# A decoder layer on one core: the first token group loaded by sequence, six products ahead of it

## The chip, the core and the metric

The kernel runs on one core of a Trainium2 chip. The metric is the device time of one execution in microseconds; times are given as the median of several runs, with the lowest and the highest. The engines are named as in the profile: PE is TensorE's matrix multiply and PEld its weight load, DVE is VectorE, ACT is ScalarE, POOL is GpSimd and SP is SyncE, which issues all the DMA transfers here.

## The reference

One decoder layer over 16 sequences of 256 tokens with 512 features, all in float32. It has three parts, each with a residual and a layer norm behind it. Only the first part touches the change:

```python
xn = x * rsqrt(mean(x * x, axis=-1, keepdims=True) + EPS) * w_norm
proj = einsum('bld,td->blt', xn, W_in)
z  = proj[..., :D_INNER]                    # 1024 columns
xi = proj[..., D_INNER:2 * D_INNER]         # 1024 columns
dt = proj[..., 2 * D_INNER:2 * D_INNER + H] # 16, then B and C, 256 each
xc = conv1d(xi, w_conv)                     # 4 taps along the tokens, causal
xi = silu(xc)
dt = softplus(dt + dt_bias)
# a scan over the tokens with 16 x 16 states, driven by dt, the means of xi, B and C
y  = (scan output spread by W_h2i) * silu(z)
out = einsum('bli,di->bld', y, W_out) + residual
```

The second part is a long convolution gated by a context tensor, the third a linear layer with a choice of two out of eight low-rank updates. They follow after all groups of the first part and are the same in both kernels.

## The kernel before

The first part runs over 8 groups of 512 tokens. A group is two sequences of 256 tokens. Its input arrives in two forms: four tiles `xt` of 128 tokens (256 KB each, for the mean square), and `xnT`, the same values with features on the partitions (four chunks of 128 features, 1,024 KB), which the matrix products read. `rms` takes the sum of squares of the tiles, half of them on ScalarE and half on VectorE in the first group; GpSimd raises it to the power of -1/2; `along_tokens` spreads the result along the tokens by two TensorE products into PSUM; `normed` multiplies `xnT` by it and by the weights `wn`, one chunk after the other, on VectorE.

The products of `proj` use a Strassen-like scheme with seven products instead of eight. The left side is a pair of column blocks of a weight matrix (`w_xi`, `w_z`, `w_bc`; a pair has four loaded blocks A11, A12, A22 and one that becomes S3, 512 KB together, and the sums S1 to S4). The right side are the four quarters of `xnT`: "11" and "12" are the first two chunks for the first and the second sequence, "21" and "22" the last two. T1 to T4 (`XT`) are differences of these quarters, so each needs both sequences. `weight_sums` forms S1 to S4 on GpSimd, `first_token_sum` and `other_token_sums` form T1 to T4. In the first group the four are made by VectorE.

A pair's products accumulate in two PSUM banks `al` and `be`. `first_products` runs A11·"11", S1·T1, S2·T2 and S3·T3; then ScalarE copies the first half of `al` to `u`, and VectorE makes three sums from `u`, `al` and `be` (`first_sums`, lines 394 to 396). `last_products` adds A12·"21" onto the first half of `al`, and S4·"22" and A22·T4 onto `be`; `last_sums` follows (lines 406 to 408). Pairs are called x0 to x3 (`w_xi`), z0 to z3 (`w_z`) and b, c (`w_bc`). The loop at line 692 goes through ten pairs, x0, x1, z0, x2, z1, x3, b, c, z2, z3 in the first group. In iteration i the first products of pair i come first, then the last products of pair i - 1; VectorE then does the first sums of pair i ahead of the last sums of pair i - 1. For an x pair `finish_sums` goes on with `mixed`: four taps of the convolution for each of two blocks, the first tap of the odd block on ScalarE (line 625), everything else on VectorE (lines 627 and 629).

In the first group `decays` (softplus and exponential of dt) is spread over iterations 1 to 4. Its logarithm and the silu behind it each make ScalarE load a table. In iteration 2 these stand between the last sums of x1 and x1's `mixed`.

The order of the instructions on every engine is the order in which the code writes them (a manual schedule). Each engine works through its own list in that order and waits at semaphores. Transfers are issued by SP in the order of the code: four `xt`, `wn`, half of `xnT` by chunks, pair 0 of `w_xi`, the other half, pair 1 of `w_xi`, pair 0 of `w_z`, then the rest. There are eight semaphores for transfers, used in turn, so an issue waits for the transfer eight places before it. Three pairs' banks exist: two in `ps_s`, four in `ps_mm`.

Until the first data are there, `idle` runs products of the identity on TensorE: eight ahead of the first `along_tokens`, four after each of the two.

Of the kernel before, what the change touches and what calls it, by code (L numbers as in the profile page):

```python
# [8 lines left out]
F32 = mybir.dt.float32  # L9
AF = mybir.ActivationFunctionType  # L10
ALU = mybir.AluOpType
# [3 lines left out]
P = 128  # L15
# [10 lines left out]
GT = 512  # L26
# [46 lines left out]
def decoder_kernel(  # L73
# [142 lines left out]
    with ExitStack() as s1:  # L216
# [11 lines left out]

        def load_x(g):
            xs = []  # L230
            for t in range(TT):
# [32 lines left out]

        def weight_sums(eng, w, p):

            ins = eng.tensor_tensor(w[:, p, S1], w[:, p, S3], w[:, p, A22], ALU.add)
            eng.tensor_tensor(w[:, p, S2], w[:, p, S1], w[:, p, A11], ALU.subtract)
            eng.tensor_tensor(w[:, p, S3], w[:, p, A11], w[:, p, S3], ALU.subtract)
            eng.tensor_tensor(w[:, p, S4], w[:, p, A12], w[:, p, S2], ALU.subtract)  # L270
# [12 lines left out]
        for p in range(2, NI // 2):  # L283
# [88 lines left out]

        def begin_products(w, p, third):
# [4 lines left out]
            product(al[:, 0:S], w, p, A11, "11", start=True)  # L378
            return al, be

        def first_products(w, p, third, begun=None, between=None):

            al, be = begun or begin_products(w, p, third)
            product(be[:, 0:S], w, p, S1, "T1", start=True)
            if between is not None:
                between()
            product(al[:, S:], w, p, S2, "T2", stop=True)
            product(be[:, S:], w, p, S3, "T3", stop=True)
            return al, be

        def first_sums(al, be, to):
            u = p2.tile([P, S], F32, tag="u", name="u", bufs=3)
            nc.scalar.copy(u, al[:, 0:S])
            nc.vector.tensor_tensor(u, u, al[:, S:], ALU.add)
            nc.vector.tensor_tensor(to[3], u, be[:, S:], ALU.add)
            nc.vector.tensor_tensor(to[3], to[3], be[:, 0:S], ALU.add)
            return u

        def last_products(al, be, w, p):

            product(al[:, 0:S], w, p, A12, "21", upon=True)
            product(be[:, 0:S], w, p, S4, "22", upon=True)
            product(be[:, S:], w, p, A22, "T4", upon=True)
# [45 lines left out]

        def normed(rt, kcs=range(KD)):  # L450
            for kc in kcs:
                nc.vector.scalar_tensor_tensor(
                    xnT[:, kc, :], xnT[:, kc, :], wn[:, kc : kc + 1], rt, ALU.mult, ALU.mult
                )
# [86 lines left out]
        for w, p in ((w_xi, 0), (w_xi, 1), (w_z, 0), (w_xi, 2)):  # L541
            weight_sums(nc.gpsimd, w, p)
# [51 lines left out]
        for g in range(groups):  # L594
# [24 lines left out]

            def mixed(c):  # L620

                xi = xis[c % 4]
                acc = p2.tile([P, GB, S], F32, tag="acc", name="acc", bufs=6)
                if c % 2:
                    nc.scalar.activation(acc, xi[:, :, 3:], AF.Identity, scale=wc[:, c, 3:4])  # L625
                else:
                    nc.vector.tensor_scalar(acc, xi[:, :, 3:], wc[:, c, 3:4], None, ALU.mult)
                for k in range(2, -1, -1):
                    ins = nc.vector.scalar_tensor_tensor(  # L629
                        acc, xi[:, :, k : k + S], wc[:, c, k : k + 1], acc, ALU.mult, ALU.add  # L630
                    )
                mixes.append(ins)
                accs.append(acc)
                silus.append(acc)
# [35 lines left out]
            before = None  # L670
            begun = []

            def finish_products():
                kind, p, al, be, u, to = before
                last_products(al, be, kinds[kind], p)

            def finish_sums(between=None):
                kind, p, al, be, u, to = before
# [12 lines left out]

            for i, (kind, p) in enumerate(order):
# [5 lines left out]
                if i == 6:  # L698
                    ms = [head_means(0)]
                if g == 0 and i == 0:  # L700
                    al, be = first_products(
                        kinds[kind], p, True, None,
                        lambda: begun.append(begin_products(w_xi, order[1][1], False)),
                    )
                else:
                    al, be = first_products(
                        kinds[kind], p, i % 3 == 0, begun.pop(0) if begun else None
                    )
                if i == 8:
                    ms.append(head_means(1))  # L710
                if i == 9:
# [45 lines left out]
                if i == 8:  # L757
# [8 lines left out]
                before = (kind, p, al, be, u, to)  # L766
                if g:
# [1086 lines left out]
```

## Time and profile before

| | us |
|---|---|
| median of 3 runs (lowest to highest) | 1390.34 (1390.28 to 1390.61) |
| the profiled execution | 1390.65 |
| its span in the profile | 1388.9 |
| PE busy in the span | 1376.9 |
| DVE busy | 1185.3 |
| POOL busy | 621.9 |
| ACT busy | 450.5 |

The profile is one execution, and times in it count from the start of its span. A row of the timeline gives the start, the busy time, the engine, the line of the code, the operation, what it writes and reads with its size, and how many such instructions were merged; in brackets stands how long the engine had been idle before and what ended that. A PE product is recorded as two matmuls for each of its two chunks. A row of SPq is the issue of a transfer, not the transfer.

### The profile page before, as it was taken

To read this page: it belongs to the slowest core of one execution; us is meant where nothing else is said; L and a number is where in the kernel's file an instruction comes from. 1 tells how busy PE (TensorE), PEld (TensorE's weight loads), DVE (VectorE), ACT (ScalarE), POOL (GpSimd) and SP (SyncE) were. 2 spreads that over 40 slices of the span, in tenths; PEclk is the share of its full clock that TensorE was granted. 3 is DMA by queue.
4 is the path that set the end of the run, shared out by engine and by line. 5 is a ranking of instruction groups with operands and counts; after the bars stand their busy time and mean duration, and the time that the engine had idled before them with its cause. 6 is when DMAs were issued, how large, how long until landed. Compare 5 with 4: busy or idle time off the path is not lost.

```text
span 1388.9 us, 19584 instructions
## 1 busy us (share of the span) xinstructions
PE 1376.9 (99%) x6967; PEld 933.7 (67%) x6967; DVE 1185.3 (85%) x2272; ACT 450.5 (32%) x977; POOL 621.9 (45%) x850
## 2 busy tenths in 40 slices
PE   8999999999999999999999999999999999999998
PEld 7888788788887887888887345454454544445454
DVE  6988879879788787787875899999999999999996
ACT  2424324243243242432421223332333333333322
POOL 5451021020100201101003668878888788878885
PEclk9999999999999999999999999999999999999999
DMA  8113212212112121121214654455534554354501
GB/s 309 34 39 91 64 54 37 70 38 58 39 42 62 57 56 52 41 53 40 78 24 72 77 69 63 67 69 69 71 65 63 77 76 65 66 69 61 76 28 38
DMA packets 362386, 89.48 MB, mean 64 GB/s; under 512 B 330032, under 2 KB 334512, under 8 KB 362288
## 3 DMA queue, kind: packets, MB, share of 16 engines
q1 hardware_dynamic: 362288, 88.23, 34.0%
q8 instruction: 55, 0.90, 0.3%
q14 instruction: 43, 0.35, 0.1%
HBM read 70.62 MB, written 17.58 MB: 64 GB/s over the span
## 4 chain that ended last, share of the span: by engine, by line
PE 95%; DVE 2%; POOL 1%; issue 0%; DMA 0%; ACT 0%; SPq 0%; POOLq 0%; DVEq 0%
PE mm L364 21%; PE y L1114 15%; PE s L364 14%; PE y L1129 12%; PE s L832 6%; PE mm L832 6%; PE y L1098 4%; PE be L1376 3%; PE al L1376 3%; PE gl L1321 2%; PE xm L640 1%; PE mm L789 1%; PE s L926 1%; PE mm L926 1%; PE al L1348 1%; PE yps L717 1%
## 5 line engine op out<-in xcount | busy, mean ns | idle before, releaser
L1129 PE MATMUL y<-kv 64*64 64x512 f32 x1536 | 179.6, 598 | 0.0
L1170 DVE TENSOR_TENSOR pr<-y,cT 128x1024 f32<-128x1024 f32 x124 | 146.1, 1219 | 34.2 <-PE y L1129 34.1
L193 DVE TENSOR_TENSOR kv<-tr,cT 128x1024 f32<-128x1024 f32 x128 | 149.9, 1213 | 1.8 <-ACT vT L154 1.8
L629 DVE SCALAR_TENSOR_TENSOR acc<-xi,wc,acc 128x512 f32<-128x512 f32 x192 | 143.2, 759 | 7.4 <-ACT acc L625 1.8
L1180 DVE TENSOR_REDUCE red<-pr 128x128 f32<-128x1024 f32 x126 | 147.2, 1208 | 0.1
L1129 PEld LDWEIGHTS y<-kv 64*64 64x64 f32 x1536 | 52.2, 132 | 118.6 <-issue 97.1
L1114 PE MATMUL y<-kv 128*128 128x512 f32 x272 | 128.0, 594 | 0.6 <-DVE pr L1162 0.4
L68 POOL TENSOR_TENSOR rs_a<-ve_a,nhalf 128x1 f32<-128x1 f32 x31 | 17.0, 548 | 247.2 <-DVE ve_a L66 246.9
L1114 PE MATMUL y<-kv,Td 128*128 128x512 f32 x248 | 116.5, 592 | 0.0
L425 POOL TENSOR_TENSOR rstd<-ms,nhalf 128x4 f32<-128x4 f32 (+1 forms) x9 | 8.6, 956 | 228.3 <-DVE ms L423 228.3
L1103 ACT COPY y<-y 64x512 f32<-64x512 f32 x124 | 69.2, 558 | 66.9 <-PE y L1098 64.9
L364 PE MATMUL mm<-XT,w_z 128*128 128x256 f32 x384 | 90.7, 379 | 0.0
L1114 PEld LDWEIGHTS y<-kv,Td 128*128 128x128 f32 x248 | 47.1, 190 | 59.3 <-issue 59.1
L1084 POOL TENSOR_TENSOR xs<-kv 128x512 f32<-128x512 f32 x63 | 80.1, 1272 | 0.0
L364 PEld LDWEIGHTS mm<-XT,w_z 128*128 128x128 f32 x384 | 73.0, 190 | 9.9
L1114 PEld LDWEIGHTS y<-kv 128*128 128x128 f32 x272 | 51.1, 189 | 42.0 <-ACT y L1103 17.4
L364 PE MATMUL mm<-xnT,w_z 128*128 128x256 f32 x288 | 70.7, 382 | 0.0
L1536 POOL TENSOR_TENSOR ol<-o,red 128x512 f32<-128x512 f32 (+1 forms) x32 | 39.5, 1235 | 62.9 <-DVE red L1180 62.9
L257 POOL TENSOR_TENSOR XT<-xnT 128x512 f32<-128x512 f32 x7 | 9.1, 1299 | 129.0 <-PE mm L832 129.0
L1098 PE MATMUL y<-xs,kv 128*128 128x512 f32 x124 | 64.9, 605 | 0.5 <-issue 0.2
L364 PE MATMUL s<-XT,w_xi 128*128 128x256 f32 x256 | 61.0, 380 | 1.1 <-DVE XT L260 0.5
L364 PEld LDWEIGHTS mm<-xnT,w_z 128*128 128x128 f32 x288 | 54.1, 190 | 10.0 <-issue 3.0
(336 smaller groups left out, 3064.7 us busy)
## 6 DMA issues: line engine op xcount, KB each, us to landing
cT<-in_ctxT SPq DMA_DIRECT2D x32, 384.0 KB
kv<-in_toep SPq DMA_DIRECT2D x32, 384.0 KB
xt<-in_x SPq DMA_DIRECT2D x32, 256.0 KB
spread<-both SPq DMA_DIRECT2D x32, 256.0 KB
first<-xt SPq DMA_DIRECT2D x124, 64.0 KB
vT<-first SPq DMA_DIRECT2D x31, 256.0 KB
out<-res SPq DMA_DIRECT2D x31, 256.0 KB
xnT<-in_xT SPq DMA_DIRECT2D x7, 1024.0 KB
```

The source lines that it names most:

```text
L193: last = nc.vector.tensor_tensor(kv[:, q, k * BQ : (k + NL // 2) * BQ], vT[:, q, blks].rearrange("p k (b i) -> p (k b) i", i=NH).unsqueeze ...
L364: nc.tensor.matmul(ps, w[:, p, a, kc, :], Xs[b][:, kc, :], start=start and kc == 0, stop=stop and kc == 1, skip_group_check=upon,)
L629: ins = nc.vector.scalar_tensor_tensor(acc, xi[:, :, k : k + S], wc[:, c, k : k + 1], acc, ALU.mult, ALU.add)
L832: nc.tensor.matmul(ps, own[a][c][:, n * P : (n + 1) * P], w_o[b][c], start=start and c == 0, stop=stop and c == HC - 1, skip_group_check=upon,
L1084: return nc.gpsimd.tensor_tensor(xs[:, q], moving(kv, q, 0), moving(kv, q, 1), ALU.add)
L1098: nc.tensor.matmul(seed, T[:, SHARED_AT, :], xs[:, q], start=True, stop=True)
L1103: nc.scalar.copy(bank_of(y, 2)[b : b + HP], seed[a : a + HP])
L1114: nc.tensor.matmul(bank_of(y, lb), w, moving(kv, q, mb), start=not late and lb not in begun, stop=False, skip_group_check=True,)
L1129: return nc.tensor.matmul(bank_of(y, lb)[cols], T[rows, DIAGONAL_AT, (b - a) * HP : (b - a + 1) * HP], moving(kv, q, lb)[rows], start=star ...
L1170: nc.vector.tensor_tensor(pr.rearrange("p (k b j) i -> p k b j i", k=2, j=NH), y[i].rearrange("p k (b j i) -> p k b j i", j=NH, i=NH), cT[ ...
L1180: nc.vector.tensor_reduce(red[:, q, 2 * i : 2 * i + 2, :].rearrange("p k t -> p (k t)"), pr, AX.X, ALU.add)
L1376: nc.tensor.matmul(ps, a[:, kc, :], w[:, kc, :], start=(start and kc == 0), stop=(kc == 1), skip_group_check=True,)
```

## The change

The first group's tokens are loaded one sequence after the other: two `xt`, the first sequence's half of `xnT` (all four chunks), then A11 and A12 alone of the pairs x0 and x1, then the other two `xt`, A11 and A12 of z0, the second half of `xnT`, and the remaining blocks of the three pairs. The first sequence is scaled as soon as its own mean squares are there. A11·"11" and A12·"21" of x0, x1 and z0 need nothing else and are run in front; ScalarE copies `u` between the two. The idle products are eight and two.

S1 of x1 is formed by VectorE after T4, and S2, S3, S4 of x1 by VectorE after the first sums of x0; GpSimd leaves these four out. In iteration 1 the last products of x0 stand between S1·T1 and S2·T2 of x1. In iteration 2 the odd block's first tap (`scaled`) stands on ScalarE ahead of the two table loads.

```diff
-        xs_next = load_x(0)
+        halves = [slice(b * S, (b + 1) * S) for b in range(GB)]
+        xs_next = load_x(0, range(TT // GB))
+        nc.sync.dma_start(xnT[:, :, halves[0]], xTg[:, :, halves[0]])
         wn = wp.tile([P, KD], F32, name="wn")
         nc.sync.dma_start(wn, w_norm)
...
-        nc.sync.dma_start(xnT[:, 0:2], xTg[:, 0:2, 0:GT])
-        nc.sync.dma_start(w_xi[:, 0, 0:4], Wxi[:, 0])
-        nc.sync.dma_start(xnT[:, 2:4], xTg[:, 2:4, 0:GT])
-        nc.sync.dma_start(w_xi[:, 1, 0:4], Wxi[:, 1])
-        nc.sync.dma_start(w_z[:, 0, 0:4], Wz[:, 0])
+        for p in range(2):
+            nc.sync.dma_start(w_xi[:, p, 0:2], Wxi[:, p, 0:2])
+        xs_next += load_x(0, range(TT // GB, TT))
+        nc.sync.dma_start(w_z[:, 0, 0:2], Wz[:, 0, 0:2])
+        nc.sync.dma_start(xnT[:, :, halves[1]], xTg[:, :, halves[1]])
+        for w, src, p in ((w_xi, Wxi, 0), (w_xi, Wxi, 1), (w_z, Wz, 0)):
+            nc.sync.dma_start(w[:, p, 2:4], src[:, p, 2:4])
...
-        rt = ps_t.tile([P, GT], F32, tag="tr", name="rt")
+        rts = [ps_t.tile([P, S], F32, tag="tr", name="rt") for _ in range(GB)]
         idle(WARM)
-        for b in range(GB):
-            along_tokens(
-                rt[:, b * S : (b + 1) * S], rms(xs_next[b * TT // GB : (b + 1) * TT // GB], True)
-            )
-            idle(WARM // 2)
-        normed(rt, (0, 1))
+        along_tokens(rts[0], rms(xs_next[: TT // GB], True))
+        idle(2)
+        normed(rts[0], range(KD), halves[0])
+        early = []
+
+        def begin(w, p):
+            al, be = begin_products(w, p, not early, True)
+            early.append((al, be, kept(al)))
+
+        def go_on(w, p, n):
+            product(early[n][0][:, 0:S], w, p, A12, "21", upon=True)
+
+        begin(w_xi, 0)
+        rstd = rms(xs_next[TT // GB :], True)
+        begin(w_xi, 1)
+        go_on(w_xi, 0, 0)
+        begin(w_z, 0)
+        along_tokens(rts[1], rstd)
+        go_on(w_xi, 1, 1)
+        go_on(w_z, 0, 2)
+        normed(rts[1], (0, 1), halves[1])
         first_token_sum(nc.vector)
-        normed(rt, (2, 3))
+        normed(rts[1], (2, 3), halves[1])
         other_token_sums(nc.vector)
-        for w, p in ((w_xi, 0), (w_xi, 1), (w_z, 0), (w_xi, 2)):
+        first_weight_sum(nc.vector, w_xi, 1)
+        for w, p in ((w_xi, 0), (w_z, 0), (w_xi, 2)):
             weight_sums(nc.gpsimd, w, p)
...
             def finish_sums(between=None):
-                kind, p, al, be, u, to = before
+                kind, p, al, be, u, to, _ = before
                 last_sums(al, be, u, to, AF.Silu if kind == "z" else AF.Copy)
+                odd = None
                 if between is not None:
+                    odd = scaled(2 * p + 1)
                     between()
...
                 if kind == "x":
                     mixed(2 * p)
-                    mixed(2 * p + 1)
+                    mixed(2 * p + 1, odd)
...
-                if g == 0 and i == 0:
-                    al, be = first_products(
-                        kinds[kind], p, True, None,
-                        lambda: begun.append(begin_products(w_xi, order[1][1], False)),
-                    )
-                else:
-                    al, be = first_products(
-                        kinds[kind], p, i % 3 == 0, begun.pop(0) if begun else None
-                    )
+                begun = early.pop(0) if early else None
+                soon = g == 0 and i == 1
+                al, be = first_products(
+                    kinds[kind], p, i % 3 == 0, begun and begun[:2],
+                    finish_products if soon else None,
+                )
...
-                if before is not None:
+                if before is not None and not soon:
                     finish_products()
                 to = places(kind, p)
-                u = first_sums(al, be, to)
+                u = first_sums(al, be, to, begun and begun[2])
+                if g == 0 and i == 0:
+                    other_weight_sums(nc.vector, w_xi, 1)
```

`kept` is ScalarE's copy of the first half of `al` to `u`, taken out of `first_sums`; `scaled` is the first tap, taken out of `mixed`; `last_products` leaves A12·"21" out where it has been run in front; `normed` takes a range of tokens.

More of the change, by code (lines that the diff above doesn't have):

```diff
@@ L227, in decoder_kernel, with load_x @@
         groups = NTOK // GT
-        def load_x(g):
+        def load_x(g, ts=range(TT)):
             xs = []
-            for t in range(TT):
+            for t in ts:
                 xt = xp.tile([P, D], F32, tag="xt", name="xt")
@@ L263, in other_token_sums, with first_weight_sum, other_weight_sums @@
             eng.tensor_tensor(Xs["T4"], Xs["21"], Xs["T2"], ALU.subtract)
-        def weight_sums(eng, w, p):
-            ins = eng.tensor_tensor(w[:, p, S1], w[:, p, S3], w[:, p, A22], ALU.add)
+        def first_weight_sum(eng, w, p):
+            return eng.tensor_tensor(w[:, p, S1], w[:, p, S3], w[:, p, A22], ALU.add)
+        def other_weight_sums(eng, w, p):
             eng.tensor_tensor(w[:, p, S2], w[:, p, S1], w[:, p, A11], ALU.subtract)
@@ L270, in weight_sums @@
             eng.tensor_tensor(w[:, p, S4], w[:, p, A12], w[:, p, S2], ALU.subtract)
-            return ins
-        xs_next = load_x(0)
+        def weight_sums(eng, w, p):
+            ins = first_weight_sum(eng, w, p)
+            other_weight_sums(eng, w, p)
+            return ins
+        halves = [slice(b * S, (b + 1) * S) for b in range(GB)]
+        xs_next = load_x(0, range(TT // GB))
+        nc.sync.dma_start(xnT[:, :, halves[0]], xTg[:, :, halves[0]])
         wn = wp.tile([P, KD], F32, name="wn")
@@ L371, in product, with begin_products @@
                 )
-        def begin_products(w, p, third):
+        def begin_products(w, p, third, closed=False):
             al, be = [
@@ L377, in begin_products @@
             ]
-            product(al[:, 0:S], w, p, A11, "11", start=True)
+            product(al[:, 0:S], w, p, A11, "11", start=True, stop=closed)
             return al, be
@@ L386, in first_products, with kept, first_sums @@
                 between()
-            product(al[:, S:], w, p, S2, "T2", stop=True)
+            product(al[:, S:], w, p, S2, "T2", stop=True, upon=begun is not None)
             product(be[:, S:], w, p, S3, "T3", stop=True)
             return al, be
-        def first_sums(al, be, to):
+        def kept(al):
             u = p2.tile([P, S], F32, tag="u", name="u", bufs=3)
             nc.scalar.copy(u, al[:, 0:S])
+            return u
+        def first_sums(al, be, to, u=None):
+            u = u or kept(al)
             nc.vector.tensor_tensor(u, u, al[:, S:], ALU.add)
@@ L397, in first_sums, with last_products @@
             return u
-        def last_products(al, be, w, p):
-            product(al[:, 0:S], w, p, A12, "21", upon=True)
+        def last_products(al, be, w, p, whole=True):
+            if whole:
+                product(al[:, 0:S], w, p, A12, "21", upon=True)
             product(be[:, 0:S], w, p, S4, "22", upon=True)
@@ L448, in load_along_tokens, with normed @@
             )
-        def normed(rt, kcs=range(KD)):
+        def normed(rt, kcs=range(KD), tokens=slice(0, GT)):
             for kc in kcs:
+                part = xnT[:, kc, tokens]
                 nc.vector.scalar_tensor_tensor(
-                    xnT[:, kc, :], xnT[:, kc, :], wn[:, kc : kc + 1], rt, ALU.mult, ALU.mult
+                    part, part, wn[:, kc : kc + 1], rt, ALU.mult, ALU.mult
                 )
@@ L618, in decoder_kernel, with scaled @@
             Bs, Cs = [], []
-            def mixed(c):
+            def scaled(c):
                 xi = xis[c % 4]
@@ L627, in mixed @@
                     nc.vector.tensor_scalar(acc, xi[:, :, 3:], wc[:, c, 3:4], None, ALU.mult)
+                return acc
+            def mixed(c, acc=None):
+                xi = xis[c % 4]
+                acc = acc or scaled(c)
                 for k in range(2, -1, -1):
@@ L670, in decoder_kernel @@
             before = None
-            begun = []
             def finish_products():
-                kind, p, al, be, u, to = before
-                last_products(al, be, kinds[kind], p)
+                kind, p, al, be, u, to, whole = before
+                last_products(al, be, kinds[kind], p, whole)
             def finish_sums(between=None):
-                kind, p, al, be, u, to = before
+                kind, p, al, be, u, to, _ = before
                 last_sums(al, be, u, to, AF.Silu if kind == "z" else AF.Copy)
+                odd = None
                 if between is not None:
+                    odd = scaled(2 * p + 1)
                     between()
@@ L765, in decoder_kernel @@
                         next(w_sums)
-                before = (kind, p, al, be, u, to)
+                before = (kind, p, al, be, u, to, not begun)
                 if g:
```

## The prediction

> **What bounds the kernel now.** I read the page's first part, then the chain that ended last.
>
> ```profile
> PE 1376.9 (99%) x6967; PEld 933.7 (67%) x6967; DVE 1185.3 (85%) x2272; ACT 450.5 (32%) x977; POOL 621.9 (45%) x850
> ...
> PE 95%; DVE 2%; POOL 1%; issue 0%; DMA 0%; ACT 0%; SPq 0%; POOLq 0%; DVEq 0%
> ```
>
> TensorE is busy for 99% of the span and carries 95% of the chain. A change therefore pays only by what it takes from TensorE's few gaps, and costs whatever gap it opens. The waits of TensorE alone say where the gaps are; columns are total us, times, longest.
>
> ```profile
> PE rt L431 <- POOL rstd L425: 1.2, 2, 0.7
> PE s L364 <- DVE XT L260: 0.5, 1, 0.5
> PE s L364 <- DVE XT L257: 0.5, 1, 0.5
> ```
>
> With the first wait for the identity (1.8 us) this is nearly all of it, and these rows lie in the first 16 us. So the only thing to win is the start, a few us of 1389. The timeline of the first 20 us shows what sets it:
>
> ```profile
> 6.57 0.69 DVE L417 SCALAR_TENSOR_TENSOR sq<-xt 128x512 f32<-128x512 f32 x1 [1.11 <-DMA xt<-in_x]
> ...
> 8.23 0.33 SPq L288 DMA_DIRECT2D w_dt<-in_WdtT  x1
> ...
> 9.14 1.41 DVE L452 SCALAR_TENSOR_TENSOR xnT<-xnT,wn,rt 128x512 f32<-128x512 f32 x2 [1.59 <-PE rt L431]
> 9.51 0.78 SPq L291 DMA_DIRECT2D dtb<-in_dt_bias  x1
> 9.56 0.73 POOL L267 TENSOR_TENSOR w_xi<-w_xi 128x256 f32<-128x256 f32 x1 [1.22 <-DMA w_xi<-in_Wxi]
> 10.90 0.63 SPq L293 DMA_DIRECT2D A<-in_A_log  x1
> ...
> 12.18 2.89 SPq L295 DMA_DIRECT2D w_z<-in_Wz  x3
> ...
> 15.21 1.21 DVE L263 TENSOR_TENSOR XT<-xnT,XT 128x512 f32<-128x512 f32 x1
> ...
> 15.83 1.17 POOL L270 TENSOR_TENSOR w_xi<-w_xi 128x256 f32<-128x256 f32 x1
> ...
> 16.34 0.41 DVE L394 TENSOR_TENSOR u<-u,s 128x256 f32<-128x256 f32 x1
> ...
> 17.30 0.42 DVE L396 TENSOR_TENSOR xi<-xi,s 128x256 f32<-128x256 f32 x1
> ...
> 18.95 1.24 PE L364 MATMUL s<-xnT,w_xi 128*128 128x256 f32 x5
> ```
>
> Three readings. First, transfers land in queue order: from the ninth on, each issue on SP waits until the transfer eight places before it has landed. So the issues at 8.23, 9.51, 10.90 and 12.18 tell when 1,538, 2,050, 2,562 and 3,074 KB had arrived (first half of xnT, w_xi pair 0, second half of xnT, w_xi pair 1); GpSimd's first weight sum, at 9.56, agrees. Second, from the square of the last x tile (6.57) to the scaling of xnT (9.14) takes 2.57 us. Third, TensorE runs without a gap from 16.36 on; until then it waits for the DVE sums T1 to T4.
>
> The next stretch shows how little room DVE has once TensorE is running:
>
> ```profile
> 21.75 0.42 DVE L407 TENSOR_TENSOR xi<-u,s 128x256 f32<-128x256 f32 x1 [1.64 <-PE s L364]
> ...
> 34.62 0.71 ACT L625 ACTIVATE acc<-xi,wc 128x512 f32<-128x512 f32 x1
> ...
> 35.36 2.33 DVE L629 SCALAR_TENSOR_TENSOR acc<-xi,wc,acc 128x512 f32<-128x512 f32 x3 [1.75 <-ACT acc L625]
> ...
> 37.60 0.41 DVE L394 TENSOR_TENSOR u<-u,s 128x256 f32<-128x256 f32 x1
> ...
> 38.29 1.89 PE L364 MATMUL s<-xnT,w_xi 128*128 128x256 f32 x8
> ...
> 38.58 0.42 DVE L396 TENSOR_TENSOR xi<-xi,s 128x256 f32<-128x256 f32 x1
> ```
>
> At 38.29 TensorE takes up the last three products of pair x2, which write into the banks that DVE has just read: A12·"21" waits for DVE's first sum (37.60 to 38.01), S4·"22" (39.15, one product later) for the third, which ends at 39.00. The slack is 0.15 to 0.28 us. DVE itself had lost 1.75 us before that (35.36), waiting for ScalarE's tap (34.62), which stood behind two table loads.
>
> **The change, step by step.** One product is 0.86 us (three in 16.36 to 18.95).
>
> *Loads.* Eight transfers of xnT and weights replace five, of the same bytes; half of xnT and two 256-KB blocks of w_xi now stand ahead of xt 2 and 3. The last xt therefore has 2,050 KB up to and with it, which arrived at 9.48 before: 3 us later than now. The first half of xnT and wn have about the 1,026 KB that let the square of the last xt run at 6.57. w_xi's two blocks come at some 7.5 and 8.2, w_z's at 10.2, xnT's second half (2,818 KB) at 11.5. SP's three extra issues (0.45 us each) are hidden by data still queued; if the queue ran dry, they would cost 1.4.
>
> *First half of the tokens.* Squares of xt 0 and 1 and the first rt are as now, so the four scalings of the half start at 7.05 (now 8.39 + 0.71 is the second rt; the first ends at 7.03). A half-size scaling is 0.28 shorter (0.70 at 512 columns; 0.42 for a DVE sum of 256). TensorE then runs six products in front: A11 of x0, x1, z0 and A12 of the same, from 7.6 to about 13.8, with the second rt between them. ScalarE's copy of x0 now stands ahead of its square of xt 2, done by 9.7, so it is not late. The six products fill time that was idle; two idle matmuls stay of eight, and no gap of TensorE below is over 1.2 us.
>
> *Second half.* The square of xt 3 at 9.55 and 2.57 us give the scaling at 12.12 (9.14 before). Two scalings (1.44 now, 0.88 halved): T1 at 13.0. T1 0.98, two scalings 0.87, T2 1.08, T3 1.14 apart as before: T2 14.85, T3 15.93, T4 17.07, and the next DVE work 18.20 (16.34 before, +1.86).
>
> *Weight sums of x1 on DVE.* The first stands between T4 and x0's sums. No row shows one on DVE. The nearest is T4 (15.21): 1.21 us for 512 columns, with GpSimd's sum at 15.83 stretched from 0.73 to 1.17. Scaled by size this is 0.6. The Trainium skill, "SBUF — State Buffer", section "SBUF: two separate sides", says that a DVE instruction with two SBUF inputs and a GpSimd instruction reading SBUF exclude each other for the whole instruction. Then only DVE's own part shrinks: 1.21 - 0.28 = 0.93. GpSimd is busy with twelve sums from 12 to 24 us here, so I take 0.93; by the scaled row the end would be 0.33 earlier. Bounds: 0.35 and 1.15. x0's sums then start at 19.05 and end at 20.43 (17.72 before: +2.7). The three other sums (2.8 us) fit into the wait for x1's products, until 23.2; without that cover they would cost all of it. GpSimd loses four sums, which nobody waited for; it starts when w_xi 0's second block lands (3,074 KB, 12.2), and S2 is there by 14.5, needed at 16. Its later sums (w_z 1, w_xi 3) start behind the taps, up to 3.3 us later: w_z 1's first at 31, TensorE needs it after 35.
>
> *TensorE.* T3 of x0 at 17.25; T1 of x1 waits for the weight sum, 19.24; x0's S4·"22", moved up between x1's products, waits for x0's third sum: 20.54 (19.81 before). From there to x2's A12·"21" it took 18.48 us with 20 products; now 19 lie there, so 17.62: it is reached at 38.16. All six early products have bought 0.13 us.
>
> *DVE behind it.* x0's last products go ahead of x1's T2 and T3, but on DVE x1's first sums stay ahead of x0's last sums. They wait for T3 of x1 (20.54 + 4 products = 23.99), so x0's last sums begin at 25.05 (21.75 before: +3.3). What follows up to x2's first sum took 15.85 us, 1.75 of it the wait for the tap. The tap now stands ahead of both loads and that wait goes: 14.10, so 39.15 instead of 37.60. ScalarE's copy that this sum needs is late next: 35.23 + 3.3, done at 38.9, 0.25 ahead.
>
> *The new stall.* TensorE stands ready at 38.16; A12·"21" can start at 39.15 + 0.41 + 0.11 = 39.67, and S4·"22" after the third sum (39.15 + 0.98 + 0.42 + 0.11 = 40.66). It was 39.15. So TensorE is **1.5 us later** from here. DVE is late by as much, so the next slots (banks of z0 at 40.9, first sums of z1 at 43.5) keep their room, and with TensorE full to the end nothing gives the time back.
>
> Sum: span 1388.9 + 1.5 = 1390.4. The profiled execution took 1390.65, 1.75 around its span and 0.31 over the median 1390.34. So 1392.15 on its own scale, **1391.8** against the median: 0.1% slower, which is within 0.2% (2.8 us), about what a measurement of this kernel can tell from no change.
>
> **The rivals.**
> *Slower by over 0.2%: the transfers in 1-KB pieces.* Both halves of xnT are now read in runs of 1 KB instead of 2. Every us by which the last xt lands after 9.5 moves the second rt, T1 to T4, x0's sums and the stall one for one. For: no large transfer of the first 10 us has pieces so small. Against: w_o is read in 1-KB runs, and the windows show 258 to 348 GB/s from 22 to 28 us, when it was under way, against 293 to 386 from 2 to 10 us. If the 512 KB took twice their 1.4 us, the end is 1391.8 + 1.4 = 1393.2. It decides from 1.3 us of delay, x2's first sum after 40.4.
> *The gain stands.* If the weight sum costs its bound of 0.35 and DVE makes up the rest in the taps, so that x2's first sum is in time, TensorE keeps 0.13 + 0.58 = 0.7: 1389.6. Against: it would need DVE 1.5 us earlier on work whose durations the trace shows.
> *The tap brings nothing.* ScalarE's order is changed as said, but if its copy of x2 came 0.5 us later than reckoned, it would replace the tap as the wait: 1392.1; with the whole 1.75 lost, 1393.6.
>
> **How the numbers follow.** Forecast, 1391.0 to 1392.6 with the weight sum between its bounds and 0.4 for landings: 0.72. Gain stands, or half of it: 0.12, nearly all within 0.2%. Late transfers: 0.10; tap lost: 0.06, of both about three quarters over 1393.1. Range 1389.7 to 1393.4. Faster by over 0.2% would need 2.8 us, more than the start still holds without its loads: 0.02. Slower: 0.12. Same: 0.86.
>
> **What would show it.** Second scaling of xnT near 12.1; six products before 14; DVE's first weight sum near 0.9; x0's S4·"22" waiting for DVE near 20.5; no DVE wait for the tap of x1; in TensorE's waits a new row on a DVE sum of x2, 1.5 to 2.5 us. I am wrong if TensorE has no gap after 21 us, or if the last xt lands away from 9.5.

## The result, and the profile after

The changed kernel took 1392.42 us in the median of 21 runs (1391.58 to 1394.20), the kernel before 1390.61 us in 21 runs on the same chip (1390.17 to 1391.76). The ratio is 1.0015 with a 95% interval of 1.0009 to 1.0021: slower by 1.8 us, within 0.2%. In the experiments below one run of e9 (1598.07 us, granted clock 0.85) and one of the kernel before (1444.40 us) had a lower granted clock and are left out of the ratios and of e9's median. The profiled execution took 1391.98 us with a span of 1390.0, 1.1 us more than the span before.

The page's rows on busy time and on the chain that ended last:

```profile
PE 1376.8 (99%) x6955; PEld 932.9 (67%) x6955; DVE 1186.7 (85%) x2280; ACT 450.1 (32%) x977; POOL 618.4 (44%) x846
...
PE 94%; DVE 3%; issue 0%; POOL 0%; ACT 0%; POOLq 0%; DVEq 0%
```

TensorE's work is the same (1376.8 us busy against 1376.9), so the loss is in its gaps: PE's share of the chain has gone from 95% to 94%, DVE's from 2% to 3%. TensorE's waits in the changed kernel (total us, times, longest):

```profile
PE s L374 <- DVE u L408: 1.1, 1, 1.1
PE mm L374 <- DVE w_xi L266: 0.9, 1, 0.9
PE s L374 <- DVE XT L260: 0.7, 1, 0.7
...
PE rt L446 <- POOL rstd L440: 0.4, 1, 0.4
```

Before, the rows after the first identity were two waits for GpSimd's rstd (1.2) and two for T1 and T2 (0.5 each), all in the first 16 us. Now the first row is a wait of 1.15 us at 39 us, for VectorE's first sum of x2 (L408, `u`). The forecast for that row was 1.5 to 2.5 us. The second is for S1 of x1, which VectorE now makes (L266). The timeline of the start:

```profile
6.02 1.22 PE L446 MATMUL rt<-ident,rstd 128*128 128x128 f32 x4 [0.43 <-POOL rstd L440]
...
7.88 1.15 PE L374 MATMUL s<-xnT,w_xi 128*128 128x256 f32 x4
...
9.50 0.69 DVE L432 SCALAR_TENSOR_TENSOR sq<-xt 128x512 f32<-128x512 f32 x1 [0.57 <-DMA xt<-in_x]
...
11.46 0.61 PE L446 MATMUL rt<-ident,rstd 128*128 128x128 f32 x4
...
12.11 0.87 DVE L468 SCALAR_TENSOR_TENSOR xnT<-xnT,wn,rt 128x256 f32<-128x256 f32 x2 [1.63 <-PE rt L446]
12.77 1.03 PE L374 MATMUL mm<-xnT,w_z 128*128 128x256 f32 x4
13.01 0.69 DVE L257 TENSOR_TENSOR XT<-xnT 128x512 f32<-128x512 f32 x1
...
16.58 1.21 DVE L263 TENSOR_TENSOR XT<-xnT,XT 128x512 f32<-128x512 f32 x1
17.71 0.94 DVE L266 TENSOR_TENSOR w_xi<-w_xi 128x256 f32<-128x256 f32 x1
18.57 0.41 DVE L408 TENSOR_TENSOR u<-u,s 128x256 f32<-128x256 f32 x1
```

The six early products run from 7.88 to 13.80, in time that was idle. But the second scaling starts at 12.11 (9.14 before), T4 at 16.58 (15.21) and x0's first sums at 18.57 (16.34). The first row is read again further down: four small matmuls that took 0.71 us before took 1.22 here. The stretch in which the loss is fixed:

```profile
24.59 0.41 DVE L422 TENSOR_TENSOR xi<-u,s 128x256 f32<-128x256 f32 x1
...
25.25 0.48 DVE L659 TENSOR_SCALAR acc<-xi,wc 128x512 f32<-128x512 f32 x1
25.76 4.56 DVE L667 SCALAR_TENSOR_TENSOR acc<-xi,wc,acc 128x512 f32<-128x512 f32 x6
...
33.52 0.72 ACT L657 ACTIVATE acc<-xi,wc 128x512 f32<-128x512 f32 x1
34.27 1.28 ACT L498 ACT_TABLE_LOAD   x1
...
34.00 4.56 DVE L667 SCALAR_TENSOR_TENSOR acc<-xi,wc,acc 128x512 f32<-128x512 f32 x6
38.58 0.42 DVE L408 TENSOR_TENSOR u<-u,s 128x256 f32<-128x256 f32 x1
39.06 2.11 PE L374 MATMUL s<-xnT,w_xi 128*128 128x256 f32 x8 [1.15 <-DVE u L408]
...
40.04 0.73 PEld L374 LDWEIGHTS s<-xnT,w_xi 128*128 128x128 f32 x4 [0.25 <-DVE xi L410]
...
49.01 1.13 PE L374 MATMUL s<-xnT,w_bc 128*128 128x256 f32 x4
```

ScalarE's tap now stands ahead of the table load (33.52, 34.27), and VectorE's six taps run without the 1.75 us hole they had. Even so x2's first sum comes at 38.58 (37.60 before), and TensorE, ready at 39.06 - 1.15 = 37.91, waits for it, and for the third sum once more (0.25). The first product of pair b (the last row) follows at 49.01. The kernel before had it at 48.02:

```profile
48.02 1.13 PE L364 MATMUL s<-xnT,w_bc 128*128 128x256 f32 x4
```

So 0.99 of the 1.1 us have been lost by there, and nothing gives them back.

### The profile page after: what moved, and what is told of

Same layout as the page of the kernel before. It is cut to its first block, busy times and chain, and to the rows that moved or that the text cites. A ratio compares the mean times of both kernels' runs of the same rounds, so it can differ in the third digit from the quotient of the medians.

```text
span 1390.0 us, 19573 instructions
## 1 busy us (share of the span) xinstructions
PE 1376.8 (99%) x6955; PEld 932.9 (67%) x6955; DVE 1186.7 (85%) x2280; ACT 450.1 (32%) x977; POOL 618.4 (44%) x846
## 4 chain that ended last, share of the span: by engine, by line
PE 94%; DVE 3%; issue 0%; POOL 0%; ACT 0%; POOLq 0%; DVEq 0%
PE mm L374 20%; PE y L1152 15%; PE s L374 13%; PE y L1167 12%; PE s L870 6%; PE mm L870 6%; PE y L1136 4%; PE be L1414 3%; PE al L1414 3%; PE gl L1359 2%; PE xm L678 1%; PE mm L827 1%; PE s L964 1%; PE mm L964 1%; PE al L1386 1%; DVE acc L667 1%
## 5 line engine op out<-in xcount | busy, mean ns | idle before, releaser
L68 POOL TENSOR_TENSOR rs_a<-ve_a,nhalf 128x1 f32<-128x1 f32 x31 | 16.9, 546 | 248.0 <-DVE ve_a L66 247.6
L374 PE MATMUL mm<-XT,w_xi 128*128 128x256 f32 x256 | 60.7, 379 | 0.9 <-DVE w_xi L266 0.9
```

What stands on the lines that cost most here:

```text
L374: nc.tensor.matmul(ps, w[:, p, a, kc, :], Xs[b][:, kc, :], start=start and kc == 0, stop=stop and kc == 1, skip_group_check=upon,)
```

## The experiments

Each kernel is the changed kernel with the edit shown, except where it says "before". The kernel before had medians of 1390.79, 1390.72 and 1390.64 us in the three sets of runs (e1 to e4, e5 to e8, e9 to e12). The three sets ran on three different chips, each beside the kernel before; the changed kernel was not run again with them. "x0's first sums", "x0's last sums" and "x2's first sum" are the starts on VectorE in the profiled execution.

Two things limit what can be read. The intervals of nearly all ratios below overlap that of the changed kernel (1.0009 to 1.0021); only e3's lies above it and e5's below. The readings therefore rest on single profiled executions, and in these the loads land at different times though their order is the same: the square of the last `xt` started at 9.50 in the changed kernel, and at 9.01 (e3), 9.79 (e2), 9.82 (e1), 9.93 (e4) and 10.04 (e7) in others. In e7, which only adds two idle products at the start, the second scaling came 0.50 later than in the changed kernel, x2's first sum 0.53 later and the span is 0.5 longer. So the landing of the last `xt` is passed on to the end, and where a few tenths matter the distance from the second scaling (12.11 in the changed kernel) is given too.

**e1: the sums of x1 on GpSimd again.**

```diff
-        first_weight_sum(nc.vector, w_xi, 1)
-        for w, p in ((w_xi, 0), (w_z, 0), (w_xi, 2)):
+        for w, p in ((w_xi, 0), (w_xi, 1), (w_z, 0), (w_xi, 2)):
...
-                if g == 0 and i == 0:
-                    other_weight_sums(nc.vector, w_xi, 1)
```

> The changed kernel with all four weight sums of x1 back on GpSimd, between those of x0 and z0; all else as changed. Theory (VectorE's chain sets TensorE's place): the first weight sum (0.94 us in the profile) no longer stands between T4 and x0's sums, so x0's first sum starts near 17.7 instead of 18.57, x2's first sum near 37.7 instead of 38.58, and TensorE's wait there (1.15 us) moves forward with it: the span is 0.8 to 0.9 us shorter than the changed kernel's 1390.0. Rival (the later landing of the last xt alone sets the delay, VectorE's sums are hidden): no change within 0.2 us.

Measured: 1392.17 us (13 runs, 1391.41 to 1393.62), ratio to before 1.0011 (1.0003 to 1.0019), span 1389.7. x0's last sums came at 23.99, 0.60 earlier than in the changed kernel; x2's first sum at 38.56, 0.02 earlier. Counted from the second scaling (12.38 here) these are 0.87 and 0.29. Either way 0.58 was given back in between. GpSimd, which has four sums more, is now still at work on w_xi 2 when VectorE does the taps of x0. The timeline of e4 (below) shows this at its clearest; in e1 the taps took 0.69 and 4.91 us where the changed kernel has 0.48 and 4.56. So the delay of x0's sums by the first weight sum is real and of the size expected, but taking it away alone is worth 0.3 us of span, not 0.8: GpSimd's four sums were not free where they were.

**e2: last products of x0 behind all of x1's first products, as before.**

```diff
-                soon = g == 0 and i == 1
+                soon = False
```

> The changed kernel with x0's last products put back behind all first products of x1. Theory: TensorE no longer waits for x0's third sum at 20.0, T2 and T3 of x1 come 1.7 us earlier, VectorE does x1's first sums in that time and waits only for T4 of x0; x0's last sums start 0.4 to 0.8 us earlier than 24.59, and x2's first sum with them. Span 0.4 to 0.8 shorter than 1390.0. Rival (moving x0's last products forward is what lets the taps of x0 start, so undoing it delays them): x0's last sums later than 24.59, span 0.5 or more longer.

Measured: 1392.05 us (21 runs, 1391.56 to 1394.36), ratio 1.0012 (1.0005 to 1.0018), span 1389.8. x2's first sum came at 38.39, 0.19 earlier, and the span was shorter by as much: half of the smallest gain expected. Part of this is the load: counted from the second scaling (12.36 here), x0's last sums came 0.47 earlier and x2's first sum 0.44, at the low end of the 0.4 to 0.8 expected. From its timeline:

```profile
24.37 0.42 DVE L422 TENSOR_TENSOR xi<-u,s 128x256 f32<-128x256 f32 x1 [0.77 <-PE s L374]
```

VectorE was done with x1's first sums at 23.60 (24.67 in the changed kernel), but x0's last products now stand behind x1's on TensorE, and VectorE waits 0.77 us for them. That wait takes back most of what the order gives.

**e4: both together.**

> Both of the first two edits in one: x1's weight sums on GpSimd, and x0's last products behind x1's first. Theory: the two shares add up, 1.3 to 2.3 us less than the changed kernel's span, so 1387.7 to 1388.7, at or under the kernel before (1388.9). Rival (the loads set the delay): the same as the changed kernel.

Measured: 1391.29 us (13 runs, 1390.61 to 1392.12), ratio 1.0004 (0.9996 to 1.0012), span 1389.1. From its timeline, to be held against the two tap rows at 25.25 and 25.76 shown above:

```profile
22.62 0.42 DVE L422 TENSOR_TENSOR xi<-u,s 128x256 f32<-128x256 f32 x1 [0.85 <-PE s L374]
...
23.29 0.71 DVE L658 TENSOR_SCALAR acc<-xi,wc 128x512 f32<-128x512 f32 x1
...
24.04 5.61 DVE L666 SCALAR_TENSOR_TENSOR acc<-xi,wc,acc 128x512 f32<-128x512 f32 x6
24.55 1.17 POOL L270 TENSOR_TENSOR w_xi<-w_xi 128x256 f32<-128x256 f32 x1
25.69 1.17 POOL L271 TENSOR_TENSOR w_xi<-w_xi 128x256 f32<-128x256 f32 x1
...
29.56 0.41 DVE L408 TENSOR_TENSOR u<-u,mm 128x256 f32<-128x256 f32 x1
```

x0's last sums are 1.97 us earlier than in the changed kernel (22.62 against 24.59), and 2.36 counted from the second scaling (12.50 here). From the first tap to z0's first sum VectorE then took 29.56 - 23.29 = 6.27 us, against 30.24 - 25.25 = 4.99 there: 1.28 is given back, 0.69 remains, and x2's first sum is at 37.90. The GpSimd rows beside the taps show why: 1.17 us each instead of the 0.73 of one left alone, and six taps 5.61 instead of 4.56. The two engines hold each other up there. The span is 0.9 us shorter than the changed kernel's, where 1.3 to 2.3 were expected.

**e3: the tap behind the table loads, as before.**

```diff
-                    odd = scaled(2 * p + 1)
```

> The changed kernel with ScalarE's tap of x1 put back behind the two table loads. Theory: VectorE waits for the tap again, about 1.8 us, x2's first sum comes near 40.4 instead of 38.58, and TensorE's wait for it grows from 1.15 to about 3 us: span 1.7 to 1.9 longer, 1391.8. Rival (VectorE has room here, the tap is hidden): the wait shows on VectorE, the span stays within 0.3.

Measured: 1395.95 us (5 runs, 1395.48 to 1397.58), ratio 1.004 (1.0027 to 1.0052), span 1393.0, which is 3.0 more than the changed kernel. From its timeline, and below it a row of its windows (stretch and length, then busy time and instructions of PE, PEld, DVE, ACT and POOL, then the granted clock of TensorE, DMA share and GB/s):

```profile
37.91 2.33 DVE L667 SCALAR_TENSOR_TENSOR acc<-xi,wc,acc 128x512 f32<-128x512 f32 x3 [1.99 <-ACT acc L657]
...
40.62 1.65 PE L374 MATMUL s<-xnT,w_xi 128*128 128x256 f32 x3 [3.12 <-DVE u L408]
```

```profile
40.00:46.00 6.00, 5.38 (x18) 4.50 (x19) 5.69 (x14) 3.35 (x6) 5.53 (x8) 0.72 0.00 0
```

The wait for the tap is back with 1.99 us, and TensorE's wait grows by the same, 1.15 to 3.12. That is about the 1.8 that was expected. The rest is the clock: the granted clock is 0.72 over these 6 us, which is half speed for 3.4 of them (0.28 of 6, doubled). The two products at 40.62 took 3.41 us from start to start, against 1.95 in the changed kernel, so the clock cost 1.46. With the 1.97 of waiting that is 3.4; the loads of this execution came 0.4 earlier, which leaves the 3.0 of its span. The medians of the spans, 1393.7 and 1390.4, differ by 3.3. The tap's place is thus worth 3.0 to 3.4 us in the changed kernel, where the next experiment finds nothing for it in the kernel before.

**e5: before, with the tap ahead of the loads and nothing else.**

```diff
                 if between is not None:
+                    odd = scaled(2 * p + 1)
                     between()
```

> The kernel before, with only ScalarE's tap of x1 moved ahead of the two table loads. Theory (TensorE bounds, and VectorE was just in time in the kernel before): VectorE's wait of 1.75 us goes, x2's first sum comes near 35.9 instead of 37.60, but TensorE takes up x2's last products at 38.3 as before: the time stays within 0.3 us of before. Rival (the tap is a gain of its own): 1 us or more less than before.

Measured: 1390.88 us (13 runs, 1390.21 to 1391.49), ratio 0.9999 (0.9991 to 1.0007), span 1388.6. From its timeline:

```profile
35.60 0.42 DVE L394 TENSOR_TENSOR u<-u,s 128x256 f32<-128x256 f32 x1
...
38.02 1.24 PE L364 MATMUL s<-xnT,w_xi 128*128 128x256 f32 x5
```

x2's first sum comes 2.0 us earlier than before (37.60), and TensorE gets to its products at 38.02 as it would have anyway: it is 0.27 earlier, as was all of this run from x0's first sums on (16.07 against 16.34). The sum is done at 36.02, so VectorE has 1.9 us to spare here. The changed kernel spends that room, and more, on the later start of its chain.

**e6 and e7: the idle products.** e6 has none ahead of the first products; e7 has ten instead of eight ahead of the first `along_tokens`.

```diff
-        idle(WARM)
+        idle(WARM + 2)     # e7; e6 has neither idle(WARM) nor idle(2)
```

> The changed kernel without the ten idle products. Theory on the changed kernel's scatter (7 of 21 runs lie 1.9 us above the rest): TensorE's clock is at half speed until it has been busy for a while; with no idle products the six products in front run at half speed (1.7 us each instead of 0.86), the second rt, which stands behind four of them, comes 1 to 3 us later than 11.46, and the end moves by as much: 1393 to 1395 us in most runs. Rival (the clock has nothing to do with the scatter): the second rt at 11.5, 1392.4 as the changed kernel.

> The changed kernel with ten instead of eight idle products ahead of the first rt, so that TensorE is busy without a gap from 1.8 to the first rt. Theory on the scatter (late clock at the start): the runs at 1393.8 and more go, all lie between 1391.5 and 1393. Rival (the scatter comes from the clock falling after the wait at x2's last products, or from elsewhere): a fifth to a third of the runs still lie 1.9 us above the others.

Measured for e6: 1393.84 us (9 runs, 1393.63 to 1395.28), ratio 1.0024 (1.0014 to 1.0033), span 1393.0. From its timeline:

```profile
7.93 2.05 PE L374 MATMUL s<-xnT,w_xi 128*128 128x256 f32 x4 [0.75 <-DMA w_xi<-in_Wxi]
9.77 1.91 PE L374 MATMUL mm<-xnT,w_xi 128*128 128x256 f32 x4
11.47 1.92 PE L374 MATMUL s<-xnT,w_xi 128*128 128x256 f32 x4
13.18 1.24 PE L374 MATMUL mm<-xnT,w_z 128*128 128x256 f32 x4
14.26 0.61 PE L446 MATMUL rt<-ident,rstd 128*128 128x128 f32 x4
```

Three products and a part of the fourth ran at half speed, and the second `along_tokens` (L446), which stands behind four of them in TensorE's order, starts at 14.26 instead of 11.46. From there every step of the chain is later by about 3 us, to the end of this execution; the median of the nine spans, 1391.9, is 1.5 above that of the changed kernel.

Measured for e7: 1392.42 us (21 runs, 1391.95 to 1393.29), ratio 1.0012 (1.0006 to 1.0019), span 1390.5. The median is that of the changed kernel, but the spread is not. The 21 spans of the changed kernel fall in two groups, 14 from 1389.5 to 1390.5 and 7 from 1391.7 to 1392.1. Two more idle products leave only the first kind (all 21 from 1390.0 to 1391.3), and no idle products only the second or worse (all nine from 1391.7 up). That points to runs in which the clock became full late: the change cut the idle products from 16 to 10, and the kernel before, with 16, has no such group in the three sets (134 spans, all from 1388.2 to 1389.8). But the changed kernel was not run beside e7, and the count is not all of it: of the other kernels with ten idle products e9 has 4 of 12 spans above a gap of 0.8 us and e2 has 3 of 21 above a gap of 1.0, but e1 and e4 have none in 13 each. No run of the upper group was profiled; that its products were slow is inferred from e6 and e7.

The profiles do show that the clock comes up at different times. Before, the first `along_tokens` was this row:

```profile
6.32 0.71 PE L431 MATMUL rt<-ident,rstd 128*128 128x128 f32 x4 [0.75 <-POOL rstd L425]
```

In the changed kernel it took 1.22 us (the first row of the timeline of the start), so it ran cold, at half speed, and so did the two idle products behind it (0.61 us in e7):

```profile
7.03 1.06 PE L543 MATMUL mm<-ident 128*128 128x128 f32 x4
```

In e1, e2 and e4, which have the same products up to there, it took 0.71. The first product, at 7.88, took 1.15 us in the changed kernel and 1.13 in e7, so there the clock was full just in time. (The clock column of the windows shows 1.00 in all of this stretch, also where products ran at half speed, so it is the durations that are read.)

**e8: the last `xt` ahead of the weight blocks.**

```diff
+        xs_next += load_x(0, range(TT // GB, TT))
...
         for p in range(2):
             nc.sync.dma_start(w_xi[:, p, 0:2], Wxi[:, p, 0:2])
-        xs_next += load_x(0, range(TT // GB, TT))
-        nc.sync.dma_start(w_z[:, 0, 0:2], Wz[:, 0, 0:2])
         nc.sync.dma_start(xnT[:, :, halves[1]], xTg[:, :, halves[1]])
+        nc.sync.dma_start(w_z[:, 0, 0:2], Wz[:, 0, 0:2])
...
+        rstd = rms(xs_next[TT // GB :])
         begin(w_xi, 0)
-        rstd = rms(xs_next[TT // GB :], True)
         begin(w_xi, 1)
+        along_tokens(rts[1], rstd)
         go_on(w_xi, 0, 0)
-        begin(w_z, 0)
-        along_tokens(rts[1], rstd)
         go_on(w_xi, 1, 1)
+        begin(w_z, 0)
         go_on(w_z, 0, 2)
```

> The changed kernel with the last two xt loaded ahead of the weight blocks (and the second half of xnT ahead of z0's block), both squares on ScalarE, and the second rt ahead of the A12 products. Theory (the landing of the last xt sets T1 to T4, x0's sums and the stall at x2): the second scaling starts near 11.0 instead of 12.11, x2's first sum near 37.6 instead of 38.58, span 0.6 to 1.0 shorter than 1390.0. Rival (x0's and x1's products on TensorE set x0's last sums): the scaling comes earlier, x2's first sum and the span stay within 0.3.

Measured: 1392.78 us (21 runs, 1390.89 to 1395.80), ratio 1.0014 (1.0008 to 1.0021), span 1392.2. From its timeline:

```profile
9.41 2.04 PE L374 MATMUL s<-xnT,w_xi 128*128 128x256 f32 x4 [2.36 <-DMA w_xi<-in_Wxi]
11.24 1.91 PE L374 MATMUL mm<-xnT,w_xi 128*128 128x256 f32 x4
12.95 1.06 PE L446 MATMUL rt<-ident,rstd 128*128 128x128 f32 x4
```

and from its windows:

```profile
7.05:8.40 1.35, 0.00 (x0) 0.00 (x0) 1.15 (x3) 0.54 (x1) 0.00 (x0) 1.00 1.01 319
8.40:8.60 0.20, 0.00 (x0) 0.00 (x0) 0.20 (x2) 0.20 (x3) 0.00 (x0) 0.77 1.04 394
8.60:15.20 6.60, 5.79 (x16) 4.84 (x17) 1.59 (x5) 1.37 (x4) 2.98 (x5) 0.50 1.04 391
```

Moving `xt` up moved `w_xi` back: the first product waits until 9.41, 2.36 us after the last idle product, and now runs at half speed, although the clock had been full before the wait (the last four idle products, at 6.44, took 0.61 us; cold, four took 1.06 in the changed kernel). The windows give the moment: the granted clock fell at 8.5, after 1.5 us of waiting, and was half for 6.8 us, until 15.3. The second `along_tokens` at 12.95 is later than in the changed kernel, not earlier. The fastest runs (1390.89, span 1389.0) may show what the order gives without the clock; none of them was profiled. So the experiment missed its question, and e10 to e12 put it again with enough idle products to bridge that wait.

**e9: VectorE takes x0's last sums and the taps of its even block ahead of x1's first sums.**

```diff
+            def half_sums():
+                kind, p, al, be, u, to, _ = before
+                last_sums(al, be, u, to, AF.Copy)
+                odd = scaled(2 * p + 1)
+                mixed(2 * p)
+                return lambda: mixed(2 * p + 1, odd)
...
+                if soon:
+                    rest = half_sums()
                 u = first_sums(al, be, to, begun and begun[2])
...
-                if before is not None:
+                if soon:
+                    rest()
+                elif before is not None:
```

> The changed kernel with VectorE's order changed alone: in iteration 1 the last sums of x0 and the taps of its even block stand ahead of the first sums of x1, the taps of its odd block behind them. Theory (x0's last sums were late only because x1's first sums, which wait for T3 of x1, stood ahead of them): x0's last sums start near 22.2 instead of 24.59, x0's taps end 1.2 us earlier, x2's first sum near 37.4 instead of 38.58, span 0.9 to 1.2 shorter than 1390.0. Rival (the order on VectorE is neutral, what counts is its sum of work): x2's first sum within 0.3 of 38.58.

Measured: 1391.85 us in the median of 12 runs (1391.35 to 1393.30), ratio 1.0011 (1.0003 to 1.002). In the profile TensorE's products took 1.18 us instead of 1.03, so only VectorE's stretch is read from it: from x0's first sums (19.05) to x2's first sum (38.32), without an idle row, it took 19.27 us, against 20.01 in the changed kernel. The order is worth 0.7 us on VectorE (0.9 to 1.2 expected); the time is 0.6 lower, which the intervals cannot tell from no change.

**e10 to e12: the parts together.** All three have the loads and order of e8 and twenty idle products (`idle(WARM + 2)`, `idle(10)`). e10 adds the edits of e1 and e2, e11 that of e9, e12 those of e9 and e1.

> The loads and TensorE order of e8 with the edits of e4, and ten idle products before and ten behind the first rt, so that TensorE has no gap until its first product. Theory: the clock stays up, the second scaling starts near 11.0, x2's first sum 1.3 us earlier than in e4 (37.90), near 36.7, span 1387.6 to 1388.4, which is 0.5 to 1.2 under the kernel before (1388.9), and the runs keep within 1 us. Rival (TensorE's own products from 9 us on set x0's last sums): 1388.5 to 1389.

> The loads and TensorE order of e8 with the idle products of e10 and VectorE's order of e9; the weight sums of x1 stay on VectorE. Theory: fewer collisions with GpSimd than in e10, x0's last sums near 21: x2's first sum near 36.6, span 1387.8 to 1388.6. Rival: the first weight sum (0.94) in the way gives it all back, 1389.

> As e11, with the weight sums of x1 on GpSimd. Theory: 0.9 us off VectorE and TensorE ahead of x0's sums, 0.5 of it given back by taps that collide with GpSimd (as e1 showed): span 1387.5 to 1388.3, the shortest of all. Rival: GpSimd's sums are late for x1's products, 1388.5 or more.

Measured: 1390.90 (1390.46 to 1391.33), 1390.91 (1390.45 to 1391.46) and 1390.82 us (1390.43 to 1391.52), 13 runs each; ratios to before 1.0002 (0.9994 to 1.001), 1.0002 (0.9994 to 1.0011) and 1.0001 (0.9993 to 1.001). The loss of the change is gone and its two groups of runs too, but none is faster than the kernel before: the spans were 1388.9, 1389.1 and 1389.1 in the profiles, where 1387.5 to 1388.6 were expected. What the six early products can do is seen in e10, from its timeline:

```profile
9.11 1.03 PE L374 MATMUL s<-xnT,w_xi 128*128 128x256 f32 x4
...
10.84 0.61 PE L446 MATMUL rt<-ident,rstd 128*128 128x128 f32 x4
...
22.57 0.42 DVE L422 TENSOR_TENSOR xi<-u,s 128x256 f32<-128x256 f32 x1 [0.85 <-PE s L374]
...
38.30 2.11 PE L374 MATMUL s<-xnT,w_xi 128*128 128x256 f32 x8 [1.60 <-DVE u L408]
```

TensorE stood ready for x2's last products at 38.30 - 1.60 = 36.70, 1.6 us ahead of the kernel before. It starts them when that did (38.29), because VectorE's sum was not there. And e10's second `along_tokens` is still at 10.84 (8.39 before): it waits behind two products whose weights come at 9.1, because the loads ahead of them hold `xt` now. The rival named for e10 came true as well: its second scaling is 1.02 us earlier than in e4 (11.48 against 12.50), but x0's last sums start at 22.57 (22.62 in e4), since VectorE waits there for TensorE. TensorE's six early products start later with their weights, and x1's products start at 18.06 (18.11 in e4). Loading `xt` earlier thus only changes which engine is late. The kernels side by side:

| | x0's first sums | x2's first sum | between | VectorE's waits in it | TensorE ready |
|---|---|---|---|---|---|
| before | 16.34 | 37.60 | 21.26 | 4.36 (1.75 of it for the tap) | 38.29 |
| e5 | 16.07 | 35.60 | 19.53 | 2.62 | 38.02 |
| changed | 18.57 | 38.58 | 20.01 | 1.34 | 37.91 |
| e1 | 18.00 | 38.56 | 20.56 | 3.39 | 37.32 |
| e4 | 18.12 | 37.90 | 19.78 | 1.81 | 36.74 |
| e10 | 17.60 | 37.82 | 20.22 | 2.39 | 36.70 |
| e11 | 18.68 | 37.96 | 19.28 | 0 | 38.15 |
| e12 | 17.70 | 37.95 | 20.25 | 2.46 | 38.12 |

"Between" starts with x0's first sums, which need T1 to T4 and so both sequences. It is 19.3 to 20.6 us in all kernels that load by sequence, but not for one reason. Where VectorE makes the sums of x1 (changed, e11) it has 18.7 and 19.3 us of work and waits little; where GpSimd makes them it has 17.2 to 18.0 us of work and waits 1.8 to 3.4 us for TensorE's products. To use e10's 1.6 us, x2's first sum would have to start at 36.2, and x0's first sums 19.3 to 20.2 us ahead of that, at 16.0 to 16.9; they came at 17.60. In e11 and e12 TensorE is held up instead: in e11, as in the changed kernel, it waits for the first weight sum on VectorE and for x0's third sum (0.26 and 0.17 us); in e12 it waits for x0's third sum and 0.55 us for x1's, which VectorE does later. None of the orders that were run brings both engines there early; whether another could is open.

## Why the prediction was right

The mechanism is the one forecast: TensorE waits at x2's last products for VectorE, whose chain started later, and nothing gives the time back. The measured 1392.42 lies 0.6 above the 1391.8. By its own steps (predicted, then measured in the profiled execution):

| step | predicted | measured |
|---|---|---|
| square of xt 3; second scaling | 9.55; 12.12 | 9.50; 12.11 |
| T1, T2, T3, T4 | 13.0, 14.85, 15.93, 17.07 | 13.01, 14.52, 15.45, 16.58 |
| six products done | 13.8 | 13.80 |
| first weight sum on DVE | 0.93 long | 0.94 long |
| x0's first sums; S4·"22" of x0 | 19.05; 20.54 | 18.57; 20.06 |
| x0's last sums | 25.05 | 24.59 |
| TensorE ready for x2's A12·"21" | 38.16 | 37.91 |
| x2's first sum; A12·"21"; S4·"22" | 39.15; 39.67; 40.66 | 38.58; 39.06; 40.04 |
| later from there | 1.5 | 0.9 to 1.0 |
| span | 1390.4 | 1390.0 |

- *Loads.* The rival of late 1-KB pieces fell: the square of the last xt started 0.05 from the forecast. That closeness is partly luck: with the same order of loads it started anywhere from 9.01 to 10.04 in other profiles.
- *T1 to T4.* The sum copied the spacing of before, 4.07 us from T1 to T4. It was 3.57: T1 took 0.69, not 1.06, as it began just when a GpSimd sum had ended, and T2 1.00, not 1.16. Of this, 0.46 is left at x0's last sums, and with 0.11 that VectorE saved behind them it is all of the difference at x2's first sum. On TensorE only 0.25 of it is left at 37.91, since the way there from x0's S4·"22" took 17.85, not 17.62.
- *The weight sum on VectorE.* By the row scaled by size it would have been 0.6; by the estimate that rests on the Trainium skill, "SBUF — State Buffer", section "SBUF: two separate sides", 0.93. It was 0.94, beside GpSimd's sum at 17.31 (1.05 us). A sum of the same size at 19.88, when GpSimd's sum before it had just ended, took 0.42. That agrees with the exclusion, and e1 confirms the delay that followed.
- *"GpSimd loses four sums, which nobody waited for."* True of TensorE, but not the whole price. With these sums GpSimd reaches the taps of x0 and stretches them by 0.56 us in e1 and 1.28 in e4. The change avoids that; the prediction gave it no credit and reckoned VectorE's stretch from a row of before.
- *The tap.* The 1.75 us were removed as forecast, and the rival in which ScalarE's copy takes the place of the wait did not come: the copy was at 38.20, done 0.03 before VectorE wanted it (0.25 forecast). e5 shows that alone the move is worth nothing, e3 that without it the change would have cost 3.0 to 3.4 us more.
- *The idle products, costed at nothing.* This is the term that was missed. "No gap of TensorE below is over 1.2 us" held, but the question was whether the clock is full by 7.9 us at all. A third of the runs lie 1.9 us higher, and e6 and e7 make the clock the likely reason, though no such run was profiled. From the profiled span to the median of spans of all runs (1390.0 to 1390.4) that makes 0.4.
- *From the profiled span to the median.* +1.1 in the profiled span, 0.4 for the upper group, and 0.25 outside the span, which was 2.04 us (median of the difference of time and span) where the kernel before had 1.79; the prediction had carried 1.75 over unchanged. What makes the 0.25 no run shows; the time outside the span was 1.98 or more in e6 to e9 and 1.81 to 1.83 in e10 to e12. Together 1.75 of the 1.8 measured. The stall was over-sized by 0.5 and these two terms, 0.65, were left out; the errors partly cancelled, and to that extent the nearness of the number is luck.

## What to carry to other kernels

Before work is moved into an idle stretch of the engine that bounds the kernel, write down for the next places where another engine must hand something over when each of the two will be there; here TensorE's gain of 1.6 us in e10 was worth nothing, because VectorE's chain began 1.3 us later than before. An operand that needs both halves of the data (T1 to T4) is set by the later half, so loading by halves helps only what needs one half. Products that keep TensorE's clock up are part of the schedule: when they are cut, ask whether the clock will still be full at the first product that others wait behind. And before a few tenths are read from two profiles, compare when their loads landed.

## What the runs showed of the hardware

- How long TensorE may wait before its clock falls is not one number here. In e8 the granted clock fell 1.5 us after the last idle product (at 8.5) and was half for 6.8 us; in e3 it fell 2.9 us into the wait (at 40.4) and was half for 3.4 us. Yet after waits of 1.15 (changed), 1.60 (e10) and 1.71 us (e1) it was still full. The Trainium skill, "TensorE: Matmul & The Clock Gate", section "Part 1: The HAM clock gate (the "warmup" mystery)", puts the fall after at least one idle window of about 3.4 us. By that rule neither wait would have been long enough; the measurements decide, for these two waits. The half speed of 3.4 us in e3 and 6.8 us in e8 agrees with one and two windows of that length.
- How late the clock becomes full differs from run to run of one kernel: 14 of 21 spans in one group and 7 in another about 1.9 us above it, with ten idle products; one group with twelve, in another set of runs. In the profiles with eight idle products in front, the first `along_tokens`, near 6 us, ran at full speed in e1, e2 and e4 (0.71 us) and cold in the changed kernel (1.22). The same section says that the window runs freely and the start of full speed varies by it.
- VectorE and GpSimd hold each other up in taps (`scalar_tensor_tensor`, two inputs in SBUF) as in sums: six taps 4.56 us alone and 5.61 with GpSimd sums beside them, GpSimd's sum 0.73 alone and 1.17 beside a tap.
